# A two-block transformer on one core: Du/dt moved to its own stream, the planner's TensorE durations replaced, output weights loaded by another stream

## The chip, the core and the metric

The kernel runs on one core of a Trainium2 chip. The metric is device time in microseconds (us), the median of several executions. Besides these there is one profiled execution, whose trace gives a start and a length for each instruction. The engines are TensorE (PE; its weight loads are shown as PEld), VectorE (DVE), ScalarE (ACT), GpSimd (POOL) and SyncE (SP), which issues most of the DMA transfers.

## The reference

A batch of 16 sequences of 256 tokens with 256 features goes through two blocks, all in float32:

```
x = x + attn0(cross(x, side, embed))       # 16 heads of 16, causal, rotary
x = x + ffn0(x @ W[category] + b)          # both sides rounded to 4-bit blocks
x = x + attn1(dudt(x))                     # 16 heads of 64, segments of 128
x = x + moe(cond2(x))                      # 8 experts, 2 of them for a token, 1 shared
```

The change lies in the third line. `dudt` is a reaction-diffusion step on the 256x256 array of one sequence, and `attn1` begins with an RMS norm of its result:

```
du_dt = zX * lap_x(y) + zY * lap_y(y) + zR * y * (1 - y)
x = du_dt * rsqrt(mean(du_dt^2) + eps) * g_norm
q, k, v = split(x @ W_qkv);  q, k = rotary(q), rotary(k)
k, v = concat(persistent, segment)         # 16 + 128 keys
out = softmax(q k^T / 8, causal) v  ->  out @ W_out
```

## The kernel before

The program has two parts. `woven` (line 292) computes the first three lines of the reference for all 16 sequences ("batches", b = 0 to 15), `mixture` (line 1034) then the fourth. The first part hands each sequence over through DRAM (`xd`), and the second starts with its own weights and an order of its own.

**How the order of the first part comes about.** Every stage is a Python generator that yields one instruction at a time. `weave` (line 182) holds them all, and in each step emits the instruction that could start earliest by its own reckoning: the time when the engine is free, and when the operands are written and the buffers read, with 0.15 us (`HOP`) between engines and 4.5 us (`LANDING`) after a DMA. An instruction of PE that comes from another stream than the one before it is put 0.1 us (`TURN`) later. At equal starts the place of the stream in the list decides, then the cost. The durations come from `Unit.cost` (line 164). What comes out is one fixed order for each engine; the chip then runs each engine's queue in this order, with semaphores between them. So a duration in `Unit.cost` doesn't change any instruction, only the order.

A stream may also yield a condition (a `lambda`); it stands still until counters in `g.done` allow it. And it may ask for a PSUM buffer (`Want`, through `single` or `pair`); there are four single banks (`g.singles`) and two pairs of banks (`g.pairs`), and the stream gives them back when their contents have been read.

**The streams of the first part.**
- `stage_a` (341): loads, cross attention, heads of attn0 and the scores' maximum. It may load batch b+1 when `b + 1 < L + 5`, where L counts the batches that are entirely done: there are five buffers for x.
- `stage_e` (380): exponentials, values and output of attn0.
- `stage_gate`, `stage_up`, `stage_down` (713 to 739): quantize the weights once, at the start.
- `stage_f` (600): ffn0; sets `F` to b+1 when a batch is done.
- `stage_p` (798): first loads and tables; then for each batch Du/dt (`diffuse`, 860) and four times `project4` (897), for groups of four heads: queries, keys, values and the rotary step.
- `stage_g` (935): `scores4` (955), the scores and the softmax of a group.
- `stage_v` (943): `values4` (988), transposes of the probabilities, the values, the output projection with `wo`, and the sum into x. Sets `V`, the number of groups done, and stores a finished batch (`L`).

Groups are counted through: i = 4 b + n. `project4` of group i waits for `i < V + 3`, `scores4` of group i for `P > i` and `V > i - 2`. `diffuse` makes `zT`, the normalized and transposed Du/dt, which all four groups of a batch read. It takes one single bank for the product with the matrix `lap`, has three operations on POOL and five on DVE up to the sum `u`, two squares on ACT, a power on POOL, two scalings on DVE, four transposes into another single bank and two copies on ACT into `zT`. In line 885 `zT` has one buffer. `project4` loads `wq` (two DMAs, two buffers), `wv` (two buffers) and `wo` (three buffers), and hands `wo` on through `scores4` to `values4`.

Of the kernel before, what the change touches and what calls it, by code (L numbers as in the profile page):

```python
# [19 lines left out]
P = 128  # L20
# [114 lines left out]
def row_size(ap):  # L135
    return math.prod(ap.shape[1:])
# [9 lines left out]
class Unit:  # L146
# [17 lines left out]
    def cost(self, fn, outs, ins):  # L164
        if self.name == "SP":
            return 0.06
        if self.name == "PE":
            if fn == "transpose":
                return 0.15
            lhsT, rhs = ins  # L170
            fp32 = 4 if rhs.dtype == F32 else 1
            rows, cols, n = lhsT.shape[0], row_size(lhsT), row_size(rhs)
            side = (2 if rows <= 32 else 1) * (3 if cols <= 32 else 2 if cols <= 64 else 1)
            return max((2 if fp32 == 4 else 1) * cols / 2070, fp32 * n / 2070 / side) + 0.01
        fixed, each = COSTS[self.name]
        n = max(row_size(x) for x in outs[:1] + ins)
        if fn == "reciprocal":
            each = 0.006
        return fixed + each * n + (0.3 if len(outs) > 1 else 0)
# [112 lines left out]
def woven(k):  # L292
    nc, tc = k.nc, k.tc
    with ExitStack() as ctx:
        g = Stages()
        g.k, g.a, g.B, g.ident = k, k.a, k.B, k.ident
        g.pe, g.dve, g.act = Unit("PE", nc.tensor), Unit("DVE", nc.vector), Unit("ACT", nc.scalar)
        g.pool, g.sp = Unit("POOL", nc.gpsimd), Unit("SP", nc.sync)
        pool = lambda name, bufs, **kw: ctx.enter_context(tc.tile_pool(name=name, bufs=bufs, **kw))
        g.w = pool("w", 1)  # L300
        g.xp = pool("x", 5)
        g.a_, g.f_, g.l_ = pool("sa", 1), pool("sf", 1), pool("sl", 1)
        space = bass.MemoryType.PSUM
        psum = pool("psum", 1, space=space)
        g.pairs = [psum.tile([P, 2, 512], F32, name=f"pair{i}") for i in range(PAIRS)]
        g.singles = [psum.tile([P, 512], F32, name=f"single{i}") for i in range(8 - 2 * PAIRS)]
        g.live, g.kT = {}, {}
        g.x, g.io, g.done = {}, {}, {"W": 0, "A": 0, "M": 0, "E": 0, "F": 0, "P": 0, "G": 0, "V": 0, "L": 0}
        with tc.manual_schedule():
            weave([stage_a(g), stage_e(g), stage_gate(g), stage_up(g), stage_down(g), stage_f(g), stage_g(g), stage_p(g), stage_v(g)])  # L310


def load(g, pool, name, shape, src):
# [484 lines left out]
def stage_p(g):  # L798
    k, a = g.k, g.a
    yield lambda: g.done["A"] > 0 and g.done["W"] == 3  # L800
    g.lap, op = load(g, g.w, "lap", [P, 2, S], a["lap"])
    yield op
    g.z = []
    for n in ("condB_zX", "condB_zY", "condB_zR"):
        t, op = load(g, g.w, n, [P, g.B], a[n].unsqueeze(0).to_broadcast([P, g.B]))
        g.z.append(t)
        yield op
    g.gn, op = load(g, g.w, "g", [P, 2], a["g"])
    yield op
    g.cos1, op = load(g, g.w, "cos1", [P, S], a["cos1"])  # L810
    yield op
    g.sin1, op = load(g, g.w, "sin1", [P, S], a["sin1"])
    yield op

    g.pmo = g.w.tile([P, 2, D], F32, name="pmo")
    pmv = tile_l(g, [P, 2, 2, 2 * P], "wq", 2)
    yield g.sp.dma_start(out=pmv, in_=a["pmv"].rearrange("p c (r w) -> p c r w", r=2))
    for c in range(2):
        wo = tile_l(g, [P, 4, D], "wq", 2)
        yield g.sp.dma_start(out=wo, in_=a["w_out1"][:, 4 * c : 4 * c + 4, :])  # L820
        pmvT = tile_l(g, [P, 4, P], "f_pT", 3)
        one = yield from single(g, pmv)
        pt = one.rearrange("p (i t) -> p i t", i=4)
        for i in range(4):
            yield g.pe.transpose(pt[:, i, :], pmv[:, c, i // 2, (i % 2) * P : (i % 2 + 1) * P], g.ident)
        yield copy_(g, pmvT, pt)
        g.singles.append(one)
        one = yield from single(g, pmvT, wo)
        pm = one[:, :D]
        yield from mm_(g, pm, [(pmvT[:, i, :], wo[:, i, :]) for i in range(4)])  # L830
        yield copy_(g, g.pmo[:, c, :], pm)
        g.singles.append(one)

    g.cosq, g.sinq = g.w.tile([P, S], F32, name="cosq"), g.w.tile([P, S], F32, name="sinq")
    yield g.pool.tensor_scalar(g.cosq, g.cos1, DH1**-0.5, None, ALU.mult)
    yield g.pool.tensor_scalar(g.sinq, g.sin1, DH1**-0.5, None, ALU.mult)


    g.keys = []
    for n in range(4):  # L840
        pmk = tile_l(g, [P, 2, 4 * PM], "pmk", 2)
        yield g.sp.dma_start(out=pmk, in_=a["pmk"][:, n])
        t = g.w.tile([P, 2, 2, PM + P], F32, name=f"keys{n}")
        for j in range(4):
            rows = row32(j, 32)
            src = pmk[rows, :, j * PM : (j + 1) * PM]
            yield g.pool.tensor_copy(t[rows, :, :, 0:PM], src.unsqueeze(2).to_broadcast([32, 2, 2, PM]))
        g.keys.append(t)
    g.mhalf = g.w.tile([P, 2], F32, name="mhalf")
    yield g.pool.memset(g.mhalf, -0.5)  # L850
    for b in range(g.B):
        yield lambda b=b: g.done["F"] > b
        zT = yield from diffuse(g, b)
        for n in range(4):
            yield lambda i=4 * b + n: i < g.done["V"] + 3
            g.live[4 * b + n] = yield from project4(g, n, zT)
            g.done["P"] += 1


def diffuse(g, b):  # L860

    zx, zy, zr = (z[:, b : b + 1] for z in g.z)
    y = g.x[b]
    one = yield from single(g, y)
    ply = one.rearrange("p (s d) -> p s d", s=2)
    for st in range(2):
        yield from mm_(g, ply[:, st, :], [(g.lap[:, c, st * P : (st + 1) * P], y[:, c, :]) for c in range(2)])
    lx, u = tile_l(g, [P, 2, D], "e_lx"), tile_l(g, [P, 2, D], "e_u")
    yield g.pool.tensor_tensor(lx[:, :, 1 : D - 1], y[:, :, 0 : D - 2], y[:, :, 2:D], ALU.add)
    yield g.pool.tensor_tensor(lx[:, :, 0:1], y[:, :, 1:2], y[:, :, 1:2], ALU.add)  # L870
    yield g.pool.tensor_tensor(lx[:, :, D - 1 : D], y[:, :, D - 2 : D - 1], y[:, :, D - 2 : D - 1], ALU.add)
    yield g.dve.tensor_scalar(u, y, -1.0, 1.0, ALU.mult, ALU.add)
    yield g.dve.scalar_tensor_tensor(u, y, zr, u, ALU.mult, ALU.mult)
    yield g.dve.scalar_tensor_tensor(lx, y, -2.0, lx, ALU.mult, ALU.add)
    yield g.dve.scalar_tensor_tensor(u, lx, zx, u, ALU.mult, ALU.add)
    yield g.dve.scalar_tensor_tensor(u, ply, zy, u, ALU.mult, ALU.add)
    g.singles.append(one)
    ms = tile_l(g, [P, 2], "e_ms", 2)
    for st in range(2):
        yield g.act.activation(lx[:, st, :], u[:, st, :], AF.Square, accum_out=ms[:, st : st + 1])  # L880
    yield g.dve.tensor_scalar(ms, ms, 1.0 / D, EPS, ALU.mult, ALU.add)
    yield g.pool.tensor_tensor(ms, ms, g.mhalf, ALU.pow)
    for st in range(2):
        yield g.dve.tensor_scalar(u[:, st, :], u[:, st, :], ms[:, st : st + 1], None, ALU.mult)
    zT = tile_l(g, [P, 2, S], "e_zT")
    one = yield from single(g, u)
    pt = one.rearrange("p (c t) -> p c t", c=2)
    for c in range(2):
        for st in range(2):
            yield g.pe.transpose(pt[:, c, st * P : (st + 1) * P], u[:, st, c * P : (c + 1) * P], g.ident)  # L890
    for c in range(2):
        yield g.act.activation(zT[:, c, :], pt[:, c, :], AF.Copy, scale=g.gn[:, c : c + 1])
    g.singles.append(one)
    return zT


def project4(g, n, zT):
# [3 lines left out]
    for which in range(2):  # L901
        cols = slice((8 * which + 2 * n) * P, (8 * which + 2 * n + 2) * P)
        yield g.sp.dma_start(out=wq[:, which], in_=a["w_qk1"][:, :, cols])
    wv, wo = tile_l(g, [P, 2, 4 * DH1], "wv", 2), tile_l(g, [P, 2, D], "wo", 3)
    yield g.sp.dma_start(out=wv, in_=a["w_v1"][:, :, n * 4 * DH1 : (n + 1) * 4 * DH1])
    yield g.sp.dma_start(out=wo, in_=a["w_out1"][:, 2 * n : 2 * n + 2, :])
    q = tile_l(g, [P, 2, S], "f_q", 3)
    by_seg = lambda t: t.rearrange("p (s t) -> p s t", s=2)
    for which in range(2):
# [16 lines left out]
        yield from mm_(g, pv[:, st, :], [(zT[:, c, st * P : (st + 1) * P], wv[:, c, :]) for c in range(2)])  # L926
    yield copy_(g, v, pv)
    g.singles.append(one)
    return q, v, wo

# [2 lines left out]
def stage_g(g):  # L935

    for i in range(4 * g.B):
        yield lambda: g.done["P"] > i and g.done["V"] > i - 2
        g.live[i] = yield from scores4(g, i % 4, *g.live[i])
        g.done["G"] = i + 1  # L940
# [11 lines left out]
            g.done["L"] = b + 1  # L952


def scores4(g, n, q, v, wo):

    keys = g.keys[n]
    prob = tile_l(g, [P, 2, 4, PM + P], "f_prob", 2)
    if n % 2 == 0:
        g.pm = tile_l(g, [P, 2, 8, PM], "f_pm", 2)  # L960
# [566 lines left out]
```

## Time and profile before

| | |
|---|---|
| median of 3 executions | 2807.39 us (2804.79 to 2811.74) |
| the profiled execution | 2814.07 us, span of its trace 2812.4 us |
| mean granted TensorE clock | 0.973 |
| instructions | 41924 |
| busy time of POOL and ACT in the span | 874.7 and 927.8 us |
| read from and written to HBM | 207.05 and 60.56 MB |

In the names of the trace, `single<-e_zT,wq` is a matmul into a single bank from the tiles `e_zT` and `wq`. A matmul of float32 with other weights than a transpose's appears as two records, each with its own weight load; a transpose appears as one. A lengthy name such as `pair<-keys,f_q` stands for all buffers of these tiles. A wait is put down to the last thing that released it. Nearly every instruction of the first part has line 160 (the helper that records operations), so that its tiles, not its line, tell what it is.

### The profile page before, as it was taken

Reading aid. Unit: us, or ns where it says so; the run is one execution under the profiler, and the core shown is the slowest. Engines: PE = TensorE matmul, PEld = TensorE weight load, DVE = VectorE, ACT = ScalarE, POOL = GpSimd, SP = SyncE. Lnnn points to the kernel's source line nnn. Section 1 sums busy time; section 2 is a strip of 40 time slices with the busy share of each in tenths; the row PEclk is TensorE's granted clock in tenths of the full one; section 3 lists DMA queues with packets and bytes.
Section 4 is the critical chain, followed back from the end, with each engine's and each line's share of the span. In section 5 each row is a group of like instructions: output and inputs, shape, how many; then the busy total and the mean of one; then the engine's idle time right before and its main releaser. Section 6 shows DMA issues by size and latency. Waiting matters only on the chain. (4 is left out here: it accounts for less than half of the span.)

```text
span 2812.4 us, 41924 instructions
## 1 busy us (share of the span) xinstructions
PE 2700.6 (96%) x15819; PEld 2034.8 (72%) x15819; DVE 1440.4 (51%) x3117; ACT 927.8 (33%) x2414; POOL 874.7 (31%) x1030
## 2 busy tenths in 40 slices
PE   5899999999999999999999998799999999999999
PEld 3667777777777777777777777655566888888866
DVE  6456766776776776776777666424340000000023
ACT  2223433334333334334434333323322222222221
POOL 4333433434434444444444343322330000000035
PEclk7789999999999999999999999899999999999999
DMA  3122221222222221231231232241112355555523
GB/s 112 57 83 76 66 84 38 93 79 64 91 90 63 87 94 55 90 96 59 88 97 39 79 94 68 65 141 46 51 38 77 126 189 196 197 197 196 197 83 105
DMA packets 196525, 270.38 MB, mean 96 GB/s; under 512 B 34912, under 2 KB 167264, under 8 KB 186976
## 3 DMA queue, kind: packets, MB, share of 16 engines
q1 hardware_dynamic: 190176, 250.87, 28.0%
q0 software_dynamic: 6144, 16.79, 2.0%
q8 instruction: 127, 2.08, 0.3%
q14 instruction: 78, 0.64, 0.1%
HBM read 207.05 MB, written 60.56 MB: 95 GB/s over the span
## 5 line engine op out<-in xcount | busy, mean ns | idle before, releaser
L160 ACT ACTIVATE f_prob<-pair,f_stat 128x144 f32<-128x144 f32 x512 | 191.2, 379 | 274.1 <-DVE f_stat L160 266.4
L160 DVE TENSOR_TENSOR pair<-pair,mask 128x256 f32<-128x256 f32 (+1 forms) x384 | 198.8, 518 | 132.9 <-PE pair L160 91.9
L1166 POOL DMA_INDIRECT got<-osort,pos_o x64 | 62.2, 972 | 628.2 <-PE bank L49 585.7
L160 PE MATMUL single<-e_zT,wq 128*128 128x256 f32 x1024 | 251.5, 389 | 2.8 <-DMA wq<-in_w_qk 1.4
L1148 ACT ACTIVATE ehT<-bank,own_b 128x256 f32<-128x256 f32 x280 | 132.9, 475 | 348.7 <-PE bank L49 348.7
L49 PE MATMUL bank<-ysT,w 128*128 128x256 f32 x1120 | 247.5, 379 | 0.2 <-ACT ysT L113 0.2
L49 PE MATMUL bank<-w,ehT 128*128 128x256 f32 x1120 | 247.5, 379 | 0.0
L49 PEld LDWEIGHTS bank<-ysT,w 128*128 128x128 f32 x1120 | 212.7, 190 | 29.4 <-ACT ysT L113 0.5
L49 PEld LDWEIGHTS bank<-w,ehT 128*128 128x128 f32 x1120 | 210.2, 190 | 27.2
L160 PEld LDWEIGHTS single<-e_zT,wq 128*128 128x128 f32 x1024 | 188.7, 192 | 39.0 <-DVE pair L160 3.3
L160 PE MATMUL pair<-keys,f_q 32*128 32x144 f32 x2048 | 162.0, 297 | 0.0
L160 PEld LDWEIGHTS pair<-keys,f_q 32*128 32x128 f32 x2048 | 134.2, 187 | 35.8 <-issue 25.2
L160 POOL TENSOR_TENSOR f_q<-f_t,f_t 128x256 f32<-128x256 f32 x128 | 91.6, 736 | 205.6 <-DVE f_t L160 201.0
L160 DVE TENSOR_TENSOR x<-x,single 128x512 f32<-128x512 f32 (+1 forms) x112 | 67.8, 605 | 161.6 <-PE single L160 157.0
L160 POOL TENSOR_SCALAR_AFFINE_SELECT b_e<-b_e 128x512 f32<-128x512 f32 x128 | 83.2, 650 | 207.0 <-ACT b_e L160 206.4
L160 ACT ACTIVATE b_e<-pair 128x768 f32<-128x768 f32 x128 | 103.7, 811 | 132.7 <-PE pair L160 106.1
L160 POOL TENSOR_TENSOR keys<-f_t,f_t 128x256 f32<-128x256 f32 x128 | 93.2, 741 | 167.5 <-DVE f_t L160 166.4
L1156 DVE TENSOR_TENSOR eo<-bank,eb 128x512 f32<-128x512 f32 x35 | 24.2, 692 | 234.4 <-PE bank L49 234.4
L160 PE MATMUL single<-wo,f_oT 128*128 128x256 f32 x512 | 131.6, 390 | 9.1 <-ACT f_oT L160 7.5
L160 DVE TENSOR_REDUCE qpad<-pair 128x2 f32<-128x256 f32 (+1 forms) x256 | 131.0, 554 | 4.4
L160 PE MATMUL pair<-b_qS,b_qkT 17*128 17x256 f32 (+1 forms) x1024 | 123.3, 363 | 5.7 <-DVE qpad L160 2.3
L160 PE MATMUL pair<-b_qkT 16*128 16x128 f32 (+1 forms) x1024 | 126.8, 368 | 1.9 <-ACT b_qkT L160 1.6
(289 smaller groups left out, 5238.5 us busy)
## 6 DMA issues: line engine op xcount, KB each, us to landing
w<-in_w SPq DMA_DIRECT2D x70, 1024.0 KB
ysort<-zero SPq DMA_DIRECT2D x32, 1024.0 KB
wq<-in_w_qk SPq DMA_DIRECT2D x128, 256.0 KB
wv<-in_w_v SPq DMA_DIRECT2D x64, 256.0 KB
wo<-in_w_out SPq DMA_DIRECT2D x64, 256.0 KB
ys<-ysort SPq DMA_DIRECT2D x35, 256.0 KB
osort<-eo SPq DMA_DIRECT2D x35, 256.0 KB
eb<-in_b SPq DMA_DIRECT2D x35, 128.0 KB
```

The source lines that it names most:

```text
L49: nc.tensor.matmul(out, lhsT, rhs, start=start and i == 0, stop=stop and i == last)
L160: return Op([(self.name, self.cost(fn, outs, aps), lambda: call(*args, **kw))], outs, aps)
L1148: nc.scalar.activation(hT[:, f, :], ph, AF.Gelu_apprx_tanh, bias=b1[:, f : f + 1])
L1156: nc.vector.tensor_tensor(o, po, b2.unsqueeze(1).to_broadcast([P, 2, D]), ALU.add)
L1166: nc.gpsimd.indirect_dma_start(out=g, out_offset=None, in_=k.osort[:, :], in_offset=bass.IndirectOffsetOnAxis(ap=r.pos_o[:, i, t : t + 1], ...
```

## The change

Three things are changed.

1. Du/dt gets a stream, `stage_d`, which stands in the list between `stage_p` and `stage_v`. It starts when the tables of `stage_p` are made (`Z`), and computes batch b when ffn0 of b is done and `stage_p` has projected all groups of batch b-2 (`P >= 4 b - 4`). `stage_p` takes `zT` from it. `zT` gets two buffers.
2. The durations of TensorE in `Unit.cost` are others. A full matmul of n columns is planned at n/570 us (before: 4 n/2070 + 0.01), a transpose at 0.12 us (0.15), matmuls with few rows or few columns of weights by rules of their own. `HOP`, `LANDING`, `TURN` and the other engines' costs stay.
3. `wo` is loaded in `scores4` instead of `project4`, and has two buffers instead of three.

```diff
             if fn == "transpose":
-                return 0.15
+                return 0.12
             lhsT, rhs = ins
-            fp32 = 4 if rhs.dtype == F32 else 1
-            rows, cols, n = lhsT.shape[0], row_size(lhsT), row_size(rhs)
-            side = (2 if rows <= 32 else 1) * (3 if cols <= 32 else 2 if cols <= 64 else 1)
-            return max((2 if fp32 == 4 else 1) * cols / 2070, fp32 * n / 2070 / side) + 0.01
+            rows, cols, t = lhsT.shape[0], row_size(lhsT), row_size(rhs) / 570
+
+            if rows <= 64:
+                return max(0.155 if rows <= 32 else 0.19, t / 2)
+            return max(t / 3.5, 0.08) if cols <= 32 else max(t / 2, 0.13) if cols <= 64 else t
...
-            weave([stage_a(g), stage_e(g), stage_gate(g), stage_up(g), stage_down(g), stage_f(g), stage_g(g), stage_p(g), stage_v(g)])
+            weave([stage_a(g), stage_e(g), stage_gate(g), stage_up(g), stage_down(g), stage_f(g), stage_g(g), stage_p(g), stage_d(g), stage_v(g)])
...
     yield g.pool.memset(g.mhalf, -0.5)
+    g.done["Z"] = 1
     for b in range(g.B):
-        yield lambda b=b: g.done["F"] > b
-        zT = yield from diffuse(g, b)
+        yield lambda b=b: g.done["D"] > b
+        zT = g.zT.pop(b)
         for n in range(4):
...
+def stage_d(g):
+
+    yield lambda: g.done["Z"]
+    for b in range(g.B):
+        yield lambda b=b: g.done["F"] > b and g.done["P"] >= 4 * b - 4
+        g.zT[b] = yield from diffuse(g, b)
+        g.done["D"] = b + 1
...
-    zT = tile_l(g, [P, 2, S], "e_zT")
+    zT = tile_l(g, [P, 2, S], "e_zT", 2)
...
-    wv, wo = tile_l(g, [P, 2, 4 * DH1], "wv", 2), tile_l(g, [P, 2, D], "wo", 3)
+    wv = tile_l(g, [P, 2, 4 * DH1], "wv", 2)
     yield g.sp.dma_start(out=wv, in_=a["w_v1"][:, :, n * 4 * DH1 : (n + 1) * 4 * DH1])
-    yield g.sp.dma_start(out=wo, in_=a["w_out1"][:, 2 * n : 2 * n + 2, :])
...
-def scores4(g, n, q, v, wo):
+def scores4(g, n, q, v):

     keys = g.keys[n]
+    wo = tile_l(g, [P, 2, D], "wo", 2)
+    yield g.sp.dma_start(out=wo, in_=g.a["w_out1"][:, 2 * n : 2 * n + 2, :])
```

More of the change, by code (lines that the diff above doesn't have):

```diff
@@ L306, in woven @@
         g.singles = [psum.tile([P, 512], F32, name=f"single{i}") for i in range(8 - 2 * PAIRS)]
+        g.zT = {}
         g.live, g.kT = {}, {}
-        g.x, g.io, g.done = {}, {}, {"W": 0, "A": 0, "M": 0, "E": 0, "F": 0, "P": 0, "G": 0, "V": 0, "L": 0}
+        g.x, g.io, g.done = {}, {}, {"W": 0, "D": 0, "Z": 0, "A": 0, "M": 0, "E": 0, "F": 0, "P": 0, "G": 0, "V": 0, "L": 0}
         with tc.manual_schedule():
-            weave([stage_a(g), stage_e(g), stage_gate(g), stage_up(g), stage_down(g), stage_f(g), stage_g(g), stage_p(g), stage_v(g)])
+            weave([stage_a(g), stage_e(g), stage_gate(g), stage_up(g), stage_down(g), stage_f(g), stage_g(g), stage_p(g), stage_d(g), stage_v(g)])
 def load(g, pool, name, shape, src):
@@ L928, in project4 @@
     g.singles.append(one)
-    return q, v, wo
+    return q, v
 def stage_g(g):
```

## The prediction

> **What bounds the kernel now.** I read the page first, then a table of stages, then the waits of TensorE, then its timeline where it idles, and last SP's queue. Columns of the stage table: stretch in us, its length, busy us (instructions) of PE, PEld, DVE, ACT and POOL, granted clock, DMA share, GB/s.
>
> ```profile
> PE 2700.6 (96%) x15819; PEld 2034.8 (72%) x15819; DVE 1440.4 (51%) x3117; ACT 927.8 (33%) x2414; POOL 874.7 (31%) x1030
> ```
>
> ```profile
> 0.00:150.00 150.00, 110.81 (x526) 74.64 (x527) 81.94 (x168) 39.81 (x81) 59.10 (x93) 0.74 0.26 79
> 150.00:550.00 400.00, 384.49 (x2515) 282.94 (x2515) 272.46 (x541) 139.06 (x383) 152.83 (x181) 0.94 0.25 77
> 550.00:1500.00 950.00, 938.68 (x6666) 713.03 (x6664) 696.45 (x1402) 367.50 (x1081) 398.96 (x464) 1.00 0.25 78
> 1500.00:1575.00 75.00, 74.72 (x539) 55.32 (x542) 55.20 (x111) 28.34 (x77) 25.48 (x31) 1.00 0.26 80
> 1575.00:1661.00 86.00, 79.37 (x526) 61.45 (x514) 57.29 (x110) 31.75 (x106) 36.23 (x42) 1.00 0.19 59
> 1661.00:1820.00 159.00, 142.10 (x1013) 114.88 (x1012) 88.74 (x179) 57.02 (x215) 57.19 (x70) 0.97 0.22 69
> 1820.00:1832.00 12.00, 0.09 (x1) 0.12 (x2) 1.10 (x5) 0.00 (x0) 1.13 (x14) 0.59 0.71 215
> 1832.00:2812.40 980.40, 970.37 (x4047) 732.43 (x4047) 187.23 (x605) 264.30 (x475) 143.75 (x137) 1.00 0.41 131
> ```
>
> TensorE sets the time. The woven part ends at 1820; the 980 us of `mixture` after it are not planned and not touched. Length less PE busy gives PE's idle time: 39.2 us up to 150, 15.5 up to 550, 11.3 in the 950 us of steady state (1.2%), 0.3 up to 1575, 6.6 up to 1661, 16.9 up to 1820, then 11.9 at the hand-over. Only idle PE time can be won, unless the order of the matmuls makes the busy time shorter.
>
> In steady state a batch takes 104.6 us. In 1575:1820 the streams A and E have run out of batches, and PE waits for the segmented attention's own chain (engine, what it worked on, what released it: us, times, longest):
>
> ```profile
> PE single L160 <- POOL f_prob L160: 11.6, 7, 5.1
> PE single L160 <- DVE f_pT L160: 2.2, 3, 1.5
> PE single L160 <- DVE f_oT L160: 1.5, 1, 1.5
> PE single L160 <- DVE e_u L160: 1.2, 1, 1.2
> PE single L160 <- ACT e_zT L160: 1.0, 2, 0.6
> ```
>
> Du/dt itself is small there; in the timeline of batch 14 it stands between two projections, and P can't go on (start, length, engine, operation, idle before it):
>
> ```profile
> 1681.75 1.89 PE L160 MATMUL single<-wv,e_zT 128*128 128x256 f32 x8
> ...
> 1683.48 1.89 PE L160 MATMUL single<-x,lap 128*128 128x256 f32 x8
> ...
> 1690.62 1.99 PE L160 MATMUL single<-wo,f_oT 128*128 128x256 f32 x8 [1.45 <-DVE f_oT L160]
> ...
> 1693.73 0.66 PE L160 MATMUL single<-ident,e_u 128*128 128x128 f32 x4
> ...
> 1694.95 0.70 PE L160 MATMUL single<-e_zT,wq 128*128 128x256 f32 x2 [0.56 <-ACT e_zT L160]
> ```
>
> From the last `wv` matmul to the next `wq` matmul are 11.3 us with nothing of P on PE.
>
> [...] a 128x256 record lasts 379 ns, the next starts 215 ns later, and weight loads fill only 72%. So an order that changes streams less often could shorten busy time too.[...] 32-row records start 6 ns apart at best (`pair<-keys,f_q`)[...].[...]
>
> **Part 1, Du/dt in a stream of its own.** No instruction is added: eight `lap` records, ten vector operations, four transposes and two `e_zT` copies a batch are issued by stage_d instead of stage_p. What it buys is what P waits for `zT` alone. P has a second gate, `i < V + 3`: group 0 of batch b needs the values of group 1 of batch b-1. Reading last `wo` matmuls of that group and first `wq` matmuls of the next batch from the timeline:
> - steady state: values end at 876.6, P starts at 879.2; at 981.5 and 984.1 likewise. Du/dt (862.8 to 873.9) lies inside the wait for the other gate. Won: 2.6 us of a chain that has slack, so nothing.
> - start: batch 1 336.2 against 341.2, batch 2 458.4 against 461.0: 5.0 and 2.6 us.
> - end: batch 13 1610.1 against 1620.2 (10.1), batch 14 1681.5 against 1695.0 (13.5), batch 15 1744.0 against 1749.1 (5.1): 28.7 us of chain.
>
> The end can't give 28.7, since PE is 90% busy. Its idle time after 1575 is 6.6 + 16.9 + 11.9 = 35.4; of this 12.4 are `mixture`'s first loads, and 5.1 the last group's scores, which nothing can cover; 18.0 remain. PE's waits beside Du/dt (1.2 for e_u, 1.0 for e_zT, the 1.5 for f_oT, whose copy stood on DVE behind an e_u operation, and 2.5 for f_prob right after it) are 6.2 and surely concerned. Between 6.2 and 18.0 I take 9. At the start I take 2 of the 15.5 idle us, since most of these belong to A, E and F (waits on qpad, d_h, c_y). What is late next: the loop of scores and values (V(i-2) frees G(i), some 47 us each way in steady state).
>
> What it may cost: the four single PSUM banks. `lap` holds one for 6.5 us and the transposes one for 1.7 us a batch; before, P held none meanwhile, afterwards it may. In 104.6 us that is 8.2 us of one bank of four: from nothing up to 1 us a batch.
>
> **Part 2, TensorE durations.** By the two formulas, a batch's PE work is planned at 113 us before (32 `wq` matmuls at 0.505, 16 each of `wo` and `wv` at 0.505, 64 `keys,f_q` at 0.149, 100 transposes at 0.15, and so on) and 101.4 after (0.449, 0.155, 0.12). Each plan adds 0.1 a change of stream, and the timeline of 550:1500 has 100 changes a batch, so 123 against 111. The trace has 104.6. The new plan is nearer, thus it expects DVE (76.7 us busy a batch) to be as tight as it is. Yet PE remains its bottleneck in both, the reachable idle time is those 11.3 us (6.2 for f_oT, 2.1 for f_pT, 1.2 for wq), and any order among the streams may come out: the bound is -11 and, if the number of changes moves by a tenth (1 us a batch), 15 us either way. I take -2.
>
> **Part 3, `wo`.** 64 loads of 256 KB move from P to G; the ring goes from three to two, which pays for the second `zT` (2 KB a partition each). Load i now waits for the values of i-2, not i-3. It is needed 29 us after its group's scores begin in steady state and 17 us at the end (timeline), so it lands in time. On SP the order matters: the queue stands still at a `wo` load until the values are read (SP waits 1151.6 us for PE in all). A `wo` of group i can now stand ahead of `wq` of group i+1, whose lead of 17 us (group 1 of a batch) shrinks to about 3, where group 2 has 4.2 to 5.4 now and PE waits up to 0.5 us for it. In steady state other streams cover it. At the end it can cost 0 to 0.5 us in about 12 groups; I take +1. Removing `wo` from P's loads saves P nothing.
>
> **Sum.** -9 - 2 - 2 + 1 = -12 on the profiled execution of 2814.07, which gives 2802. The median shown is 6.7 under that execution, so 2795.
>
> **Rivals.**
> 1. The end's idle time only moves (PE waits for f_prob through POOL's 1.9 us multiplication and the copies, not for zT): -3, 2804. For it: 11.6 of the waits name f_prob. Against: P's later start is what leaves PE without other work.
> 2. Slower. In steady state six streams and Du/dt share four single banks; P gets one while `lap` holds another, and A or F stands. At 1.5 us a batch over 12 batches that is +18, with half of the end's gain left +10 to +14: 2819. It decides from 1 us a batch on, where it eats the 12. For it: steady state repeats to 0.1 us with 1.2% idle, so a new order has more to lose than to win. Against: 8.2 us of a bank is little.
> 3. The better durations remove changes of stream: 10 fewer a batch at 0.1 us, over 15 batches -15 beside part 1: 2780. For it: changes cost 9.8 us of the 104.6 (starts later than that shape's usual). Against: changes follow from dependences, which stay.
>
> **Chances.** The forecast 0.38, rival 1 0.22, rival 2 0.27, rival 3 0.13. A measurement of this kernel tells about 0.3% (8.4 us) from no change. The forecast's own range, 2786 to 2803, lies mostly under 2799, so faster is 0.28 + 0.13 + 0.04 = 0.45; same 0.10 + 0.16 = 0.26; slower 0.27 + 0.02 = 0.29. The range takes in rivals 2 and 3: 2778 to 2821.
>
> **What would show it.** In the changed profile `lap` of a batch should start well before the last `wv` of the batch before it; in the last three batches the first `wq` should follow the values within 3 us; the woven part should end near 1808; a steady batch should still take 104 to 105 us. A steady batch over 105.6, or the woven part ending after 1820, proves the forecast wrong; one under 103 means that the order itself got better, which I don't count on.

## The result, and the profile after

The changed kernel takes 2797.27 us (median of 7, 2794.77 to 2799.78) against 2809.38 us (median of 7 of the kernel before, run along with it). The ratio is 0.9954, with a 95% interval of 0.9943 to 0.9964: 0.46% faster, 12.1 us. Its profiled execution took 2797.27 us with a span of 2795.6; that of before, 2814.07, lay 4.7 us above its median, so the two traces differ by 16.8 us where the medians differ by 12. Everything below that compares traces rests on one execution each.

First the page's busy line of the kernel after, then its stage table (stretch, length, busy us and instructions of PE, PEld, DVE, ACT, POOL, granted clock, DMA share, GB/s). The woven part now ends at 1803, so the last stretches are cut there.

```profile
PE 2688.8 (96%) x15819; PEld 2026.2 (72%) x15819; DVE 1434.2 (51%) x3111; ACT 935.0 (33%) x2420; POOL 856.4 (31%) x1030
```

```profile
150.00:550.00 400.00, 382.74 (x2504) 282.21 (x2501) 268.84 (x540) 142.28 (x394) 151.48 (x181) 0.95 0.26 79
550.00:1500.00 950.00, 933.75 (x6668) 708.30 (x6667) 692.43 (x1394) 373.02 (x1082) 384.55 (x466) 1.00 0.25 78
...
1575.00:1661.00 86.00, 83.79 (x567) 63.72 (x565) 61.68 (x120) 30.22 (x97) 34.30 (x40) 1.00 0.16 50
1661.00:1805.00 144.00, 133.89 (x972) 110.04 (x970) 83.58 (x168) 55.83 (x206) 54.33 (x65) 0.99 0.26 82
```

PE's idle time is 17.3 us in 150:550 (15.5 before), 16.3 in 550:1500 (11.3), 2.2 in 1575:1661 (6.6), and 10.1 in 1661:1805, of which some 2 belong to the hand-over. Nothing was won before 1500. To compare ends, the next rows cut both runs where batch 10 is stored and where the last output projection of the woven part ends. First the kernel before, then the changed one:

```profile
805.30:1432.00 626.70, 619.81 (x4393) 471.23 (x4392) 459.68 (x924) 240.80 (x708) 262.10 (x307) 1.00 0.25 79
1432.00:1819.10 387.10, 362.97 (x2545) 280.87 (x2544) 252.96 (x504) 142.77 (x467) 151.03 (x178) 0.99 0.24 74
```

```profile
804.40:1431.60 627.20, 616.60 (x4393) 467.68 (x4393) 456.06 (x919) 246.09 (x714) 252.02 (x307) 1.00 0.25 79
1431.60:1802.90 371.30, 357.91 (x2541) 279.14 (x2541) 254.16 (x505) 141.52 (x460) 146.43 (x174) 1.00 0.24 75
```

The six batches 5 to 10 take the same time (104.45 and 104.53 us each), and batch 10 is done at the same moment (1432.0 and 1431.6). Nearly all of what the traces differ by comes after it: 387.1 against 371.3 us, with 24.1 and 13.4 us of idle PE in them. Of these, 16.4 and 8.4 us lie in the last three batches. The waits of PE in the end stage, 1661:1805 of the kernel after, name what is left:

```profile
PE single L160 <- POOL f_prob L160: 5.5, 2, 5.1
PE single L160 <- ACT f_oT L160: 1.1, 2, 0.7
PE single L160 <- ACT f_pT L160: 0.7, 3, 0.2
```

Of the waits for f_prob in the end (11.6 us, 7 times before) the one of 5.1 us remains, the very last group's, beside one of 0.4. The waits for e_u and e_zT are gone. The timeline of PE around batch 14 of the kernel after shows why:

```profile
1678.71 1.99 PE L160 MATMUL single<-x,lap 128*128 128x256 f32 x8
...
1682.92 0.59 PE L160 MATMUL single<-pmo,f_ppT 128*128 128x256 f32 x2
1683.44 1.25 PE L160 MATMUL pair<-keys,f_q 32*128 32x144 f32 x16
1684.62 1.99 PE L160 MATMUL single<-e_zT,wq 128*128 128x256 f32 x8
...
1686.89 0.60 PE L160 MATMUL single<-ident,e_u 128*128 128x128 f32 x4
```

The `lap` product at 1678.7 is already batch 15's, and so are the transposes at 1686.9. The projection of batch 14 starts at 1684.6, 1.5 us after the values that open its gate (the `wo` matmuls that end at 1683.1); before, it started 13.5 us after them.

### The profile page after: what moved, and what is told of

It is laid out like the page before. It is cut to its first block, busy times and chain, and to the rows that moved or that the text cites. A ratio compares the mean times of both kernels' runs of the same rounds, so it can differ in the third digit from the quotient of the medians.

```text
span 2795.6 us, 41975 instructions
## 1 busy us (share of the span) xinstructions
PE 2688.8 (96%) x15819; PEld 2026.2 (72%) x15819; DVE 1434.2 (51%) x3111; ACT 935.0 (33%) x2420; POOL 856.4 (31%) x1030
## 5 line engine op out<-in xcount | busy, mean ns | idle before, releaser
L160 ACT ACTIVATE b_e<-pair 128x768 f32<-128x768 f32 x128 | 103.6, 809 | 166.1 <-PE pair L160 159.5
L160 POOL TENSOR_TENSOR f_q<-f_t,f_t 128x256 f32<-128x256 f32 x128 | 93.4, 750 | 110.3 <-DVE f_t L160 109.3
```

The lines of the kernel that those rows point to most:

```text
L160: return Op([(self.name, self.cost(fn, outs, aps), lambda: call(*args, **kw))], outs, aps)
```

## The experiments

Twelve kernels ran, each against the kernel before on the same chip, whose medians were between 2809 and 2811. "Part 1" is Du/dt's stream, "part 2" the durations, "part 3" the loads of `wo`.

### The parts, one without the other

Parts 1 and 3, with `Unit.cost` as before (the diff is against the changed kernel):

```diff
-                return 0.12
+                return 0.15
...
-            rows, cols, t = lhsT.shape[0], row_size(lhsT), row_size(rhs) / 570
-            if rows <= 64:
-                return max(0.155 if rows <= 32 else 0.19, t / 2)
-            return max(t / 3.5, 0.08) if cols <= 32 else max(t / 2, 0.13) if cols <= 64 else t
+            fp32 = 4 if rhs.dtype == F32 else 1
+            rows, cols, n = lhsT.shape[0], row_size(lhsT), row_size(rhs)
+            side = (2 if rows <= 32 else 1) * (3 if cols <= 32 else 2 if cols <= 64 else 1)
+            return max((2 if fp32 == 4 else 1) * cols / 2070, fp32 * n / 2070 / side) + 0.01
```

> Parts 1 and 3 of the change (Du/dt in its own stream, two zT buffers, wo loaded by the scores' stream), with the durations of TensorE as before. Theory of the prediction: parts 1 and 3 are -10 of the -12, so about 2799 against 2809 (ratio 0.996), and the first wq of the last three batches follows the values of the gate within 3 us. Rival, the durations made the gain: 2807 to 2811 (ratio 0.999 to 1.001).

Measured: 2912.01 us, ratio 1.0366 (1.0342 to 1.0389). 103 us slower, the other way than either theory. The first `wq` of the last three batches follows the gate's values by 5.2, 1.5 and 1.5 us: the theory was right on this for two batches of the three, and wrong on the time.

Part 2 alone (the diff of `Unit.cost`, nothing else):

> Part 2 alone: the planner's TensorE durations of the change, Du/dt within the projections' stream, wo as before. Theory: -2, between -11 and +15, ratio 0.999; the last three batches still wait for zT between 5 and 13 us. Rival, the durations made the gain: 2797 (ratio 0.9955).

Measured: 2870.64 us, ratio 1.0212 (1.0187 to 1.0237), 61 us slower, again outside both. The waits for `zT` in the last three batches stayed: 5.1, 4.7 and 15.4 us from the gate's values to the first `wq`.

Part 3 alone (the diffs of `project4` and `scores4`):

> Part 3 alone: wo loaded by the scores' stream with two buffers. Theory: +1 (0 to +6), ratio 1.000 to 1.002. Rival, that freeing P's queue of wo's wait makes the gain: below 2803 (ratio 0.998).

Measured: 2811.4 us, ratio 1.0000 (0.9989 to 1.0010). The order of TensorE's instructions is the same as before to the last one; part 3 costs nothing and gives nothing here.

Parts 2 and 3:

> Parts 2 and 3 without part 1: Du/dt stays within the projections' stream. Theory: near part 2 alone, -1 (ratio 0.9995), and the gain of the whole change is missing by 9 to 11 us. Rival, the durations or wo made the gain: 2797 to 2800 (ratio 0.9955 to 0.9965).

Measured: 2880.12 us, ratio 1.0241 (1.0218 to 1.0264), 71 us slower and outside both.

Parts 1 and 2. The room for the second `zT` comes from a small edit in the quantization of the weights:

```diff
-    amax, unit, inv, scl = small("q_amax"), small("q_unit"), small("q_inv"), small("q_scl")
+    amax, unit, scl = small("q_amax"), small("q_unit"), small("q_scl")
+    inv = small("q_inv") if scratch.__name__ == "<lambda>" else unit
```

> Parts 1 and 2 without part 3: Du/dt's stream with two zT buffers and the durations of the change, wo loaded by the projections into three buffers as before (room for the second zT is made by computing one reciprocal of the weights' quantization in place). After the first four runs the parts don't add: parts 1 and 3 gave +103, part 2 +61, all three -12. Theory that the pair of parts 1 and 2 makes a good order and part 3 only pays for memory: 2795 to 2803 (ratio 0.995 to 0.998). Rival, that the order is decided by small things and each variation is a new draw: anywhere from 2800 to 2900.

Measured: 2794.75 us, ratio 0.9939 (0.9922 to 0.9956). The intervals of this kernel and the changed one overlap, and the order of TensorE's instructions is that of the changed kernel in all but two of 15819 places. So in this setting of the planner parts 1 and 2 make the gain, and only together; the next section asks how far that goes beyond this setting.

What goes wrong with part 1 under the old durations shows in a steady batch. The rows are the kernel of parts 1 and 3, batch 5 to 10, then its batch 6 cut at changes of the granted clock:

```profile
825.80:1522.20 696.40, 655.47 (x4393) 492.91 (x4392) 458.56 (x882) 258.12 (x750) 263.90 (x307) 0.96 0.22 71
```

```profile
941.90:971.07 29.17, 27.59 (x169) 19.51 (x167) 22.82 (x45) 10.03 (x28) 12.17 (x14) 1.00 0.32 101
971.07:974.49 3.42, 3.12 (x10) 2.67 (x11) 0.98 (x2) 0.58 (x1) 0.84 (x2) 0.50 0.55 182
974.49:1001.79 27.30, 24.92 (x195) 17.47 (x194) 20.15 (x37) 10.60 (x28) 7.79 (x9) 1.00 0.00 1
1001.79:1005.21 3.42, 3.42 (x9) 2.70 (x8) 1.99 (x5) 0.83 (x4) 1.38 (x1) 0.50 0.00 0
1005.21:1035.93 30.72, 28.88 (x225) 22.09 (x223) 18.03 (x36) 13.10 (x39) 14.81 (x18) 1.00 0.33 104
1035.93:1039.34 3.41, 3.41 (x12) 2.90 (x12) 0.51 (x3) 0.84 (x2) 0.00 (x0) 0.50 0.00 0
```

Three times in each batch the granted clock (third column from the end) is halved for 3.4 us. In front of each stands a gap; the timeline of PE shows the first and the second:

```profile
969.02 0.82 PE L160 MATMUL pair<-b_qS,b_qkT 17*128 17x256 f32 x8
971.37 1.11 PE L160 MATMUL single<-ident,d_h 128*128 128x128 f32 x4 [1.53 <-POOL d_h L160]
972.27 2.99 PE L160 MATMUL single<-e_zT,wq 128*128 128x256 f32 x8
...
999.76 0.44 PE L160 MATMUL single<-ident,f_pm 128*128 128x128 f32 x2
1001.52 1.78 PE L160 MATMUL pair<-fT,a_qT 128*128 128x256 f32 x4 [1.32 <-issue]
```

PE waited 1.53 us for d_h and 1.32 us before `fT,a_qT`; eight `wq` records then take 2.99 us instead of the usual 1.99. The third, of 1.84 us, is before the transposes of `e_u` at 1035.7. The order repeats itself every 116 us, and with it the gaps. The table gives, for each run, the mean of batches 5 to 10 and the end from batch 10 on: period; idle PE a batch; time at half clock a batch (from the record of the granted clock); length of the end; idle PE in the end; length of the last three batches and idle PE in them.

| kernel | median | period | idle | half clock | end | idle in it | last three | idle in them |
|---|---|---|---|---|---|---|---|---|
| before | 2809 | 104.5 | 1.2 | 0 | 387 | 24.1 | 164.9 | 16.4 |
| after | 2797 | 104.5 | 1.8 | 0 | 371 | 13.4 | 160.4 | 8.4 |
| parts 1, 3 | 2912 | 116.1 | 6.8 | 10.2 | 391 | 22.6 | 153.3 | 8.7 |
| part 2 | 2871 | 108.8 | 4.0 | 2.8 | 397 | 24.3 | 176.3 | 15.8 |
| part 3 | 2811 | 104.7 | 1.3 | 0 | 389 | 24.6 | 166.1 | 16.2 |
| parts 2, 3 | 2880 | 110.1 | 4.1 | 5.1 | 407 | 25.6 | 192.9 | 20.7 |
| parts 1, 2 | 2795 | 104.6 | 1.8 | 0 | 374 | 13.1 | 163.0 | 8.2 |

Period less idle less half of the time at half clock is 102.8 to 104.1 in all rows (part 2: 108.8 - 4.0 - 1.4 = 103.4): the work is the same to about 1 us, and what tells the steady states apart is gaps, counted once as idle time and once more where the clock was halved after them.

### How much hangs on the order itself

A planner's constant was moved by 0.01 us in the kernel before and in the changed one:

```diff
-TURN = 0.1
+TURN = 0.11
```

> The kernel before with one planner constant moved by 0.01 us: a change of stream on TensorE costs 0.11 us in the plan instead of 0.10. No instruction changes, only the order. If orders are stable against such things: 2809 within 8 us (ratio 0.997 to 1.003). If each order is a draw: 20 to 100 us slower.

> The changed kernel with the same constant at 0.11 us. If the three parts together make orders that are good as such: 2797 within 8 us (ratio to before 0.993 to 0.999). If the -12 is the luck of one order: 2820 to 2900 (ratio 1.004 to 1.03).

Measured: before 2938.35 us (ratio 1.0455, 1.0433 to 1.0478), after 2824.47 us (1.0042, 1.0023 to 1.0060). Then 0.09 in both:

> The kernel before with a change of stream at 0.09 us in the plan. At 0.11 it was 2938 (+128). If orders are draws: 20 to 130 us slower than 2809, with one to three clock halvings in each steady batch. If 0.11 was a special case: 2809 within 8 us.

> The changed kernel with a change of stream at 0.09 us in the plan. At 0.11 it was 2824 (+27). If orders are draws: 2815 to 2900; the last three batches take 165 us or less all the same, since Du/dt is early.

Measured: 2902.78 us (1.0322, 1.0300 to 1.0344) and 2815.98 us (1.0016, 1.0007 to 1.0025). So with the constant at 0.09, 0.10 and 0.11, the kernel before takes 2903, 2809 and 2938 us, the changed one 2816, 2797 and 2824. The change is worth 87, 12 and 114 us in the three pairs. Three of the four new kernels lie in the ranges of the theory that each order is a draw, and the first lies above it (+128 where 20 to 100 were expected). Within a row of three nothing differs but the order and, for some copies out of PSUM, the engine that the plan chose (ScalarE runs 2414 instructions in the kernel before and 2440 with 0.11), so that a duration in the plan changes a little more than the order. What the 128 us of the kernel before at 0.11 are made of, in its steady state (batches 5 to 10) and in its longest waits there:

```profile
829.80:1539.30 709.50, 658.26 (x4398) 492.96 (x4397) 459.77 (x911) 245.19 (x720) 257.26 (x308) 0.95 0.22 71
```

```profile
PE single L160 <- DMA wq<-in_w_qk: 12.2, 4, 5.2
PE single L160 <- POOL d_h L160: 9.4, 7, 2.1
```

8.5 us idle and 12.0 us at half clock a batch, period 118.3 (means: its batches take from 88 to 161 us). PE waits for `wq` up to 5.2 us here, a wait that was 0.5 us at most in the kernel before.

### Du/dt in its stream, but not early

```diff
-        yield lambda b=b: g.done["F"] > b and g.done["P"] >= 4 * b - 4
+        yield lambda b=b: g.done["F"] > b and g.done["P"] >= 4 * b
```

> The changed kernel with Du/dt's stream held until the projections have finished the batch before (P >= 4 b instead of P >= 4 b - 4): stream, durations and wo stay, being early goes. Theory, being early shortens the end: the last three batches (from the end of batch 12 to that of batch 15) take 165 us or more, as in every kernel so far without an early Du/dt (165 to 193), instead of 160.5; the whole time 2806 or more, unless the steady state becomes another. Rival, the end is short because of the durations: 160 us or less, and 2797.

Measured: 2881.46 us, ratio 1.0247 (1.0224 to 1.0271). The last three batches take 194.8 us, the end holds 22.0 us of idle PE instead of 13.4, and the steady period is 109.3 us. It is the kernel of parts 2 and 3 again (2880, 192.9, 25.6, 110.1), and TensorE's order is the same as there over the first 10918 of 15819 records: a stream that may not run ahead is no stream. Between this order and the changed kernel's lie 84 us; 29 of them fall in six steady batches (655.9 against 627.2 us), where the prediction expected nothing from being early, so that these belong to the order and not to the end. About 35 lie in the end (406.6 against 371.3 us from batch 10 on): 8.7 us more of idle PE; an estimated 15 for the clock, which is halved for 34.1 us instead of 3.4; and an estimated 6 because 44 more records of TensorE lie behind that cut (2585 against 2541, at 0.14 us each). In the last three batches PE idles 18.1 us instead of 8.4. Its end still waits for Du/dt's results, 2.9 us for e_zT and e_u:

```profile
PE single L160 <- POOL f_prob L160: 8.8, 6, 5.1
PE single L160 <- DMA wq<-in_w_qk: 4.5, 3, 1.6
PE single L160 <- ACT f_pT L160: 2.3, 7, 0.8
PE single L160 <- ACT e_zT L160: 1.5, 3, 0.6
PE single L160 <- DVE e_u L160: 1.4, 2, 1.0
```

### Truer durations still

```diff
-                return 0.12
+                return 0.11
...
-            rows, cols, t = lhsT.shape[0], row_size(lhsT), row_size(rhs) / 570
+            rows, cols, t = lhsT.shape[0], row_size(lhsT), row_size(rhs) / 595
```

> The changed kernel with a full matmul of n columns planned at n/595 us and a transpose at 0.11, which is what the trace of before shows between the starts of two matmuls of one stream (215 ns a record of 256 columns, two records; 109 ns a transpose); the 0.1 us of a change of stream are then not counted twice. If truer durations give a better order: 2790 to 2797. If orders are draws: 2810 to 2900.

Measured: 2855.76 us, ratio 1.0155 (1.0133 to 1.0176). Nearer to the trace was not faster. Its end is as good as the changed kernel's (14.2 us idle, 162.6 us for the last three batches), its steady period is not (109.5, with 3.7 us idle and 6.3 at half clock).

### The price of a gap

```diff
+        for _ in range(t // 5):
+            nc.vector.tensor_copy(hT[:, 7, :], hT[:, 7, :])
         for s in range(2):
-            mm(nc, po[:, s, :], [(hT[:, f, s * P : (s + 1) * P], w2[:, f, :]) for f in range(8)])
+            mm(nc, po[:, s, :], [(hT[:, f, s * P : (s + 1) * P], w2[:, f, :]) for f in (7, 0, 1, 2, 3, 4, 5, 6)])
```

> The changed kernel, with TensorE made to wait in each expert tile t of the second part: the last block of the hidden layer is copied onto itself t // 5 times by VectorE (none for tiles 0 to 4, six times for 30 to 34), and the output matmuls begin with this block. Prices a gap on TensorE by its length. Theory,[...] a tile (14.0 us) lengthens[...] by the gap plus about 1.5 us. Rival, the clock drops for other reasons: the tile lengthens by the gap alone throughout.

Measured once: 2833.9 us. The experiment mostly missed its aim. The copies held up VectorE's copy of the next tile's input as well, so that from tile 10 on the waits fell apart into several shorter ones elsewhere in the tile (14.25 us a tile grew to some 15.5), and the clock stayed full. Only the last tile has one long gap. Timeline of PE:

```profile
2691.78 7.14 PE L49 MATMUL bank<-w,ehT 128*128 128x256 f32 x32
2698.76 5.77 PE L49 MATMUL bank<-ysT,w 128*128 128x256 f32 x26
2707.11 8.64 PE L49 MATMUL bank<-w,ehT 128*128 128x256 f32 x32 [2.58 <-issue]
```

With this gap of 2.58 us the clock was halved from 2706.7 to 2710.1 (0.51 over 2706.7:2710.2), and the same 32 records took 8.64 us instead of 7.14. That prices this one halving at 1.5 us, the estimate that was put down; what shorter gaps would have brought, the run doesn't show.

## Why the prediction was right, point by point

**The time.** Forecast 2795, faster; measured 2797.27.

**Where the gain lies.** The working had nothing in the steady state, 2 us at the start and 9 of the 18 reachable us at the end. The trace has none in the steady state (104.45 and 104.53 us a batch), none at the start (idle 1.8 us more in 150:550), and 10.7 us less of idle PE after batch 10, 8.0 of it in the last three batches. One trace tells the start only roughly: batch 4 is done at 805.3 before and 804.4 after, but at 796.6 in the kernel of part 3, whose order on TensorE is that of before. In batches 14 and 15 the first `wq` follows the gate's values by 1.5 us each, as foretold. In batch 13 it doesn't (1611.6 against 1600.9), because the projections were still at batch 12's last group until 1608.2. The woven part ends at 1802.9 (1808 was expected). The other 5 us of the end are busy time. About 3 of them are the clock's, by an estimate: after batch 10 it is halved for 10.2 us before and for 3.4 us after, and PE is busy in 8.9 and 3.2 us of these. That is no merit of the order: the kernel of parts 1 and 2 has the same order but for two places, and its trace has 10.2 us at half clock in the end. What is left, some 2 us of matmuls that follow each other faster, I can't assign to a part.

**That being early shortens the end.** The one run that takes only this away has 18.1 us of idle PE in the last three batches instead of 8.4. Over all draws, the six kernels with an early Du/dt idle 8.2 to 11.4 us there, and the seven without 12.9 to 20.8. The old durations make no exception: parts 1 and 3 idle 8.7 us there, and the 22.6 us of their whole end are so many because batches 11 and 12 still have the gaps of the steady state (13.9 us idle). So this part of the working holds with either set of durations. Not all thirteen are draws of their own: part 3 has the order of before, parts 1 and 2 that of after but for two places. The length of the last three batches separates them less well (before with 0.09 has 163.3 us), for the batches end with different amounts of work still open.

**Part 3.** +1 was booked, with `wq` behind `wo` on SP. Alone it moved no instruction of PE and 0 us (interval -3 to +3), so the wait that it was charged for didn't come.

**Where the working was wrong though its sum came out.** It priced three parts and added them: -9 and -2 for part 1, -2 for part 2, +1 for part 3. Measured one by one, parts 1 and 3 give +103, part 2 +61, part 3 nothing, and all together -12. The step that failed is the sentence on part 2 that bounds the order at "-11" and "15 us either way". Moving `TURN` by 0.01 moved the kernel before by 92 and 128 us (against its own time on the same chip). The 12 that were forecast were met because this setting of the planner drew an order without new gaps; at 0.09 and 0.11 the changed kernel takes 2816 and 2824, more than the kernel before at 0.10. That the size came out is luck in this sense. The bound took the idle time of the order at hand for all that an order can change. It holds downwards: steady batches of before had 1.2 us idle and full clock, so there was nothing to win. Upwards it doesn't hold at all.

**The rivals.** Rival 1, that the idle time only moves, is out: the waits for f_prob in the end fell from 11.6 to 5.5 us, and idle PE fell with them. Rival 3, fewer changes of stream, didn't come: in 550:1500 the tiles that TensorE works on, which stand for the streams here, change 991 times before and 1037 times after. Rival 2 foresaw what happened in the variants that lost, a steady state with more gaps, but at 1.5 us a batch; measured were 2.8 to 13.8. The cause that it named, Du/dt's stream holding single banks, can't be theirs in general: part 2 alone and the kernel before at 0.09 and 0.11 have no such stream. Whether the banks play a part where the stream exists wasn't tried.

**Whether -12 is a merit of the change.** At three values of `TURN` the changed kernel beat the kernel before each time, by 12 to 114 us. The comparison at 0.10 is the one with the best order of the three on both sides. That speaks for the sign, but three of three would come out by chance once in eight times if orders were mere draws, and the changed kernel with TensorE's durations moved by 4 to 8% is 45 us slower than the kernel before. The size of the difference is the luck of one pair. Why one order has gaps that repeat, and another none, I couldn't tell beyond naming what each gap waits for.

## What to carry to other kernels

Where a program plans the order of its own instructions, an edit to one stream or to one duration draws a new order for all, and its parts can't be priced one by one: measure each edit at two or three values of a constant that shouldn't matter, and compare the rows. Where TensorE is as busy as here, a new order has little to win and much to lose: in 550:1500 it was busy for 938.7 of 950 us before, at a granted clock of 1.00, which left 11.3 us of idle time; moving `TURN` to 0.11 cost the kernel before 128 us. Look first at the end of a pipeline, where streams have run out and the idle time hangs on one chain: there a step that runs ahead takes its wait out of the chain, and here TensorE idled less there in every order that was tried with it (8.2 to 11.4 us in the last three batches, against 12.9 to 20.8).

## What the runs showed of the hardware

In the kernel of parts 1 and 3, gaps of 1.3, 1.5 and 1.8 us within otherwise busy stretches were each followed by 3.4 us at half clock (0.50 in batch 6), in every batch from 5 to 10.

A gap of 2.48 us in two runs was not followed by the same. The kernel of part 3 has TensorE's order of before to the last record, and a gap of 2.48 us near 1691 that is the one of before near 1698. First part 3, then before:

```profile
1693.38 1.09 PE L160 MATMUL single<-ident,f_prob 128*128 128x128 f32 x4 [2.48 <-POOL f_prob L160]
1694.27 3.17 PE L160 MATMUL single<-e_zT,wq 128*128 128x256 f32 x8
```

```profile
1700.10 0.66 PE L160 MATMUL single<-ident,f_prob 128*128 128x128 f32 x4 [2.48 <-POOL f_prob L160]
1700.59 1.89 PE L160 MATMUL single<-e_zT,wq 128*128 128x256 f32 x8
```

In the first the eight `wq` records behind the gap take 3.17 us, about the 2.99 us of the eight at half clock in the kernel of parts 1 and 3, so that half clock is the reading here too. In the second they take 1.89 us, at a granted clock of 1.00 over 1697.6:1706. So the length of a gap didn't decide alone; what else did, the two traces don't show.

Matmuls with few rows overlapped across streams too. In the kernel before the 16 `keys,f_q` records of 32 rows that stand together take 968 ns (median of 126) from the first start to the last; in 12 groups of the changed kernel 6 records of attn0's heads (16 and 17 rows) stand between them, and they take 968 to 969 ns.
